# Layer 2 of the last image: its depthwise taps on the unnormalised input, in half chunks, behind layer 1's last products

## The chip, the core and the metric

One core of one Trainium2 chip runs the whole kernel. The metric is the device time of one execution in microseconds; several executions are made, and their median is compared. An execution with the hardware profiler on gives the page and the trace that this document reads; its times are microseconds from its first instruction.

## The reference, cut to what matters

Eight images x of 384 channels and 32 x 32 points go through four residual layers, `x = x + layer_k(group_norm(x))`. Layer 0 is a convolution with attention, layer 1 a mixture of four two-layer networks per point, layer 3 a deformable attention. Layer 2 is what the change touches:

```
h = (x - mean) / sqrt(var + 1e-5)          # per image, 32 groups of 12 channels
y = depthwise 3x3 convolution of h          # ternary weights, zero padding of one point
x = x + (1x1 convolution of y, 384 -> 384)  # ternary weights
```

A group's mean and variance come from all points of the image, so h is known only when the last channel of x is complete. The taps are linear: on a point inside the image, taps of h are scale times (taps of x) plus shift times (sum of the nine taps). On the border some of the taps fall on padding, which is zero in h and not in x.

## The kernel before, in words

A partition holds three channels ("chunks" c = 0, 1, 2) of 1024 points each. Everything is float32. A 128x512 product of TensorE appears in the profile as two MATMUL records.

Work of layers 1 to 3 runs as generators that are interleaved. `layer1(b)` gives a list of units: for each half h of the points (512 of them) 12 groups of three hidden products (`ph`, L1481, with Relu on ACT and a multiplication by the gate on DVE, L1467), then for each output chunk m four parts of three products into `y` (L1502). The last part of a chunk adds the result to x (L1508, DVE). While `layers(b)` (layer 2, then layer 3 of image b) runs, each of its steps yields an estimate of idle time, and units of layer 1 of image b + 1 are put in for it (UNIT = 2.6). For the last image, 7, no later image is left: its layers run against the second part of layer 3 of image 6, two of its steps for each step of the other (`following`, L1995).

`layer2` takes the statistics (`gn_start`, L101: two `bn_stats` a chunk; `gn_finish`, L138: two one-column products `gna`, L117, and `gnb`, L128, with small DVE operations and a power on GpSimd, L98), lets ACT write the normalised image h2 (`affine`, L147), and takes nine taps a chunk on DVE: the centre as `tensor_scalar` (L1569), eight as `scalar_tensor_tensor` (L1577). Then 18 products with the 1x1 weights (`pw`, L1585) and the addition to x (L1592).

`layer3` normalises x again, multiplies it (`pq`, L1622, gives q; `px`, L1645, transposes it to `xT`), takes 25 strided taps of q on DVE (`off`, L1690 and L1692; 54 operations an image and a start), a Gelu on ACT (L1697), products `pom` (L1718), tanh and the interpolation weights `wt` on ACT and GpSimd (L1753 to L1757), the sampling products `xsb` (L1761), keys `pk` (L1775) and values `pv` (L1784), six units of attention (`s` L1800, exp on ACT L1817, `pav` L1826, sums `pss` L1839, transposes and a division on DVE L1847 to L1874) and the output products `pf` (L1929).

Buffers that matter: five image buffers (`im`, 12 KB a partition each); two accumulators of two banks (`big`), three of one bank (`fbank`), one (`vbank`, used by `pav`). The instruction order on each engine is fixed when the program is built; an engine never passes a waiting instruction.

`weights23` prepares the weights of layers 2 and 3 once, in the routing stage of layer 1 (L1346 to L1371).

Of the kernel before, what the change touches and what calls it, by code (L numbers as in the profile page):

```python
# [7 lines left out]
F32 = mybir.dt.float32  # L8
AF = mybir.ActivationFunctionType
ALU = mybir.AluOpType  # L10
AX = mybir.AxisListType

B, C, H, W = 8, 384, 32, 32
N = H * W
# [41 lines left out]
def tile_kernel(ctx: ExitStack, tc: tile.TileContext, i: dict, out: bass.AP):  # L56
# [52 lines left out]
    def gn_mean(st, tag):  # L109
        mv = small.tile([P, 2], F32, tag="gn_mv", name=f"mv_{tag}")  # L110
        nc.vector.bn_aggr(mv, st.rearrange("p a b -> p (a b)"))
        return mv

    def gn_spread(mv, tag, psum):

        pg = psum(f"gna_{tag}")
        nc.tensor.matmul(pg[:, 0:2], lhsT=g4, rhs=mv, start=True, stop=True)  # L117
        ga = small.tile([P, 2], F32, tag="gn_ga", name=f"ga_{tag}")
        nc.vector.tensor_copy(ga, pg[:, 0:2])
        dm = small.tile([P, 1], F32, tag="gn_dm", name=f"dm_{tag}")  # L120
        nc.vector.tensor_tensor(dm, mv[:, 0:1], ga[:, 0:1], ALU.subtract)
        nc.vector.tensor_tensor(dm, dm, dm, ALU.mult)
        return ga, dm
# [14 lines left out]
    def gn_finish(st, tag, psum):  # L138

        return gn_scale(*gn_spread(gn_mean(st, tag), tag, psum), tag, psum)  # L140
# [1196 lines left out]
    def weights23(pl):  # L1337

        raw2 = pl.img("raw2").rearrange("p c n -> p (c n)")
        pw2 = raw2[:, : KC * C].rearrange("p (c n) -> p c n", c=KC)  # L1340
        dw2 = raw2[:, KC * C : KC * C + KC * 9].rearrange("p (c n) -> p c n", c=KC)
        nc.sync.dma_start(out=pw2, in_=i["pw2"])
        nc.sync.dma_start(out=dw2, in_=i["dw2"])
        m2 = wd.tile([P, KC], F32, name="m2")
        s2 = wd.tile([P, KC], F32, name="s2")
        nc.vector.tensor_reduce(m2, dw2, AX.X, ALU.add, apply_absolute_value=True)  # L1346
        nc.vector.tensor_scalar(m2, m2, 1.0 / 9.0, 1e-5, ALU.mult, ALU.max)
        nc.vector.reciprocal(s2, m2)
        tap2 = wd.tile([P, KC, 9], F32, name="tap2")
        ternary(tap2, dw2, [s2[:, c : c + 1] for c in range(KC)])  # L1350
        nc.vector.reciprocal(m2, s2)
        for c in range(KC):
            nc.vector.tensor_scalar(tap2[:, c, :], tap2[:, c, :], m2[:, c : c + 1], None, ALU.mult)
        mp = wd.tile([P, 1], F32, name="mp")
        sp = wd.tile([P, 1], F32, name="sp")
        nc.vector.tensor_reduce(mp, pw2, AX.XY, ALU.add, apply_absolute_value=True)
        pm = fbank("pm")
        nc.tensor.matmul(pm[:, 0:1], lhsT=ones, rhs=mp, start=True, stop=True)
        nc.vector.tensor_scalar(mp, pm[:, 0:1], 1.0 / (C * C), 1e-5, ALU.mult, ALU.max)
        nc.vector.reciprocal(sp, mp)  # L1360
        upw2 = wd.tile([P, KC, C], F32, name="upw2")
        ternary(upw2, pw2, sp)
        nc.vector.reciprocal(mp, sp)
        so3 = wd.tile([P, 1], F32, name="so3")
        bo3 = wd.tile([P, 1], F32, name="bo3")

        nc.vector.tensor_scalar(bo3, bn3[:, 4:5], 1e-6, None, ALU.add)
        rsqrt(so3, bo3, 1)
        nc.vector.tensor_tensor(so3, so3, bn3[:, 1:2], ALU.mult)
        nc.vector.tensor_tensor(bo3, bn3[:, 0:1], bn3[:, 3:4], ALU.subtract)  # L1370
        nc.vector.scalar_tensor_tensor(bo3, bo3, so3, bn3[:, 2:3], ALU.mult, ALU.add)  # L1371
        return tap2, upw2, mp, so3, bo3

# [12 lines left out]
    def third(pl, k, name):  # L1388

        return pl.one([P, KC, HALF], f"hd{k}", name)  # L1390
# [9 lines left out]
    def layer1(pl, b, late=False):  # L1400
# [95 lines left out]
        def result(h, m, part):  # L1496
            if part == 0:
                state["y"] = fbank(f"y{b}_{h}_{m}")
            y = state["y"]
            for k in range(3 * part, 3 * part + 3):  # L1500
                e, dc = divmod(k, KC)
                nc.tensor.matmul(  # L1502
                    y, lhsT=w2[:, e, dc, m * P : (m + 1) * P], rhs=state[h, k],
                    start=(k == 0), stop=(k == NE * KC - 1),
                )
            if part == 3:
                hs = slice(h * HALF, (h + 1) * HALF)
                nc.vector.scalar_tensor_tensor(  # L1508
                    xt[:, m, hs], y, yb[:, 1, m : m + 1], xt[:, m, hs], ALU.add, ALU.add
                )  # L1510

        units = []

# [33 lines left out]
                        unit((result, h, m, part))  # L1547
        return units

    def layer2(pl, b, xt):  # L1550
        last = b == B - 1
        st = None
        for c in range(KC):
            st = gn_start(xt, f"d2_{b}", c, st)
            yield 1.3
        ss = gn_finish(st, f"d2_{b}", fbank if last else vbank)
        yield 5.0
        h2 = pl.img(f"h2_{b}")
        if last:
            y = [third(pl, c, f"y_{b}_{c}").rearrange("p a n -> p (a n)")[:, :N] for c in range(KC)]  # L1560
        else:
            y = pl.img(f"y_{b}")
            y = [y[:, c, :] for c in range(KC)]
        for c in range(KC):
            affine(h2[:, c, :], xt[:, c, :], ss)
        for c in range(KC):
            src = h2[:, c, :].rearrange("p (h w) -> p h w", h=H)
            dst = y[c].rearrange("p (h w) -> p h w", h=H)
            nc.vector.tensor_scalar(dst, src, tap2[:, c, 4:5], None, ALU.mult)  # L1569
            yield 0.8  # L1570
            for t in (0, 1, 2, 3, 5, 6, 7, 8):
                dy, dx = t // 3 - 1, t % 3 - 1
                r0, r1 = max(0, -dy), H - max(0, dy)
                c0, c1 = max(0, -dx), W - max(0, dx)
                d = dst[:, r0:r1, c0:c1]
                f = src[:, r0 + dy : r1 + dy, c0 + dx : c1 + dx]
                nc.vector.scalar_tensor_tensor(d, f, tap2[:, c, t : t + 1], d, ALU.mult, ALU.add)  # L1577
                yield 1.25
        yield 3.5
        for m in range(KC):  # L1580
            whole, pw = pair(last, f"pw{b}_{m}")
            for h in range(2):
                hs = slice(h * HALF, (h + 1) * HALF)
                for c in range(KC):
                    nc.tensor.matmul(  # L1585
                        pw[h], lhsT=upw2[:, c, m * P : (m + 1) * P], rhs=y[c][:, hs],
                        start=(c == 0), stop=(c == KC - 1),
                    )
            xm = xt[:, m, :]
            outs = zip((xm[:, :HALF], xm[:, HALF:]), pw) if last else [(xm, whole)]  # L1590
            for d, f in outs:
                nc.vector.scalar_tensor_tensor(d, f, mp, d, ALU.mult, ALU.add)  # L1592
            nc.sync.dma_start(out=x2_dram[b, :, m, :], in_=xm)
            yield 0.0
# [373 lines left out]
    with pd:  # L1968
        for k, u in enumerate(units):
            u()  # L1970
            if k == 8:
                tap2, upw2, mp, so3, bo3 = weights23(pl)
        def layers(b):
            xt = xs_img.pop(b)
            yield from layer2(pl, b, xt)
            yield from layer3(pl, b, xt, put_image(b), False)

        for b in range(B - 1):
            units = layer1(pl, b + 1)
            due = 0.0  # L1980
            this = layers(b)
            for idle in this:
                if idle is None:
                    if b == B - 2:
                        break
                    continue
                due += idle
                while due >= UNIT and units:
                    units.pop(0)()
                    due -= UNIT  # L1990
            for u in units:
                u()


        following = layers(B - 1)  # L1995
        for _ in this:
            for _ in range(2):
                next(following)
        for _ in following:
            pass  # L2000
        okt = pl.flat([P, B * NU3 * 16], "okt3")
        recf = rec3.rearrange("p u q -> p (u q)")
        nc.vector.tensor_scalar(okt, recf, R_LO, None, ALU.is_ge)
        nc.vector.scalar_tensor_tensor(okt, recf, R_HI, okt, ALU.is_le, ALU.mult)
        okm = pl.one([P, 1], "okm", "okm3")
        nc.vector.tensor_reduce(okm, okt, AX.X, ALU.min)
        pok = fbank("pok3")
        nc.tensor.matmul(pok[:, 0:1], lhsT=ones, rhs=okm, start=True, stop=True)
        nc.vector.tensor_scalar(bad3, pok[:, 0:1], P - 0.5, None, ALU.is_lt)
# [163 lines left out]
```

## Time and profile before

| what | us |
|---|---|
| median of 3 runs | 3491.53 (3490.93 to 3492.99) |
| the profiled execution, its own time | 3494.72 |
| the span of its instructions | 3492.9 |
| TensorE busy (PE) | 3384.1, 97% of the span |
| VectorE busy (DVE) | 1696.7, 49% |
| ScalarE busy (ACT) | 1298.5, 37% |
| GpSimd busy (POOL) | 206.1, 6% |
| mean granted TensorE clock | 0.987 |

How to read it: PE is busy nearly all the time, so the shares over the whole span say little; what one change is worth is read in its own stage. Layer 1 of image 7 ends at 3272.85 us in this trace, layer 2 of image 7 lies between 3273 and 3333, layer 3 of images 6 and 7 fills the rest. A busy PE at half clock counts as busy: matmul records are the same in number and take twice as long.

### The profile page before, as it was taken

What the parts mean: (1) busy time and instruction counts of PE and PEld (TensorE: products, weight loads), DVE (VectorE), ACT (ScalarE), POOL (GpSimd) and SP (SyncE); (2) the same over time, 40 slices, a digit from 0 to 9 for tenths busy, and PEclk for the clock granted to TensorE, in tenths of its full rate; (3) what the DMA queues carried; (4) which work ended last, traced back from release to release, by engine and by line L of the source; (5) the groups of instructions that cost most, each with busy time, mean ns of one, the idle gap of its engine ahead of it and who ended that gap; (6) DMA issues with size and microseconds to landing.
All of it is one profiled execution on the core that took longest, in us unless ns stands there. A gap on an engine that the chain in (4) does not pass through costs nothing.

```text
span 3492.9 us, 44919 instructions
## 1 busy us (share of the span) xinstructions
PE 3384.1 (97%) x18599; PEld 1458.3 (42%) x18599; DVE 1696.7 (49%) x2881; ACT 1298.5 (37%) x1514; POOL 206.1 (6%) x231
## 2 busy tenths in 40 slices
PE   6999999999999999998999999999999999999888
PEld 2333434343434343443344445344453444534434
DVE  8942232323232323234366365663656637566573
ACT  5655544444444444433222323313233232232222
POOL 2100000000000000000000200102001020010112
PEclk9999999999999999999999999999999999999898
DMA  9972121212121212123500101101111011110000
GB/s 357 295 205 79 26 79 27 79 26 79 26 79 26 79 27 78 28 79 125 220 24 21 50 39 35 40 21 50 40 35 40 21 50 40 35 39 18 0 37 19
DMA packets 86259, 234.01 MB, mean 67 GB/s; under 512 B 21672, under 2 KB 21896, under 8 KB 79130
## 3 DMA queue, kind: packets, MB, share of 16 engines
q1 hardware_dynamic: 83882, 222.75, 19.9%
q10 hardware_dynamic: 1248, 4.72, 0.3%
q8 instruction: 150, 2.46, 0.3%
q0 software_dynamic: 912, 3.53, 0.3%
q14 instruction: 67, 0.55, 0.1%
HBM read 145.77 MB, written 75.59 MB: 63 GB/s over the span
## 4 chain that ended last, share of the span: by engine, by line
PE 41%; DVE 9%; DMA 1%; ACT 1%; POOL 0%; issue 0%; DVEq 0%; ACTq 0%; POOLq 0%; SPq 0%
PE y L1502 12%; PE ph L1481 10%; DVE y L1577 5%; PE pq L1622 4%; PE pw L1585 3%; PE pf L1929 3%; PE s L1800 2%; PE pav L1826 2%; DVE hd L1467 1%; DMA o<-o 1%; PE pk L1775 1%; PE pv L1784 1%; PE xsb L1761 1%; PE pss L1839 1%; PE plog L1231 1%; DVE off L1692 1%
## 5 line engine op out<-in xcount | busy, mean ns | idle before, releaser
L827 ACT ACTIVATE p<-s 128x1024 f32<-128x1024 f32 x512 | 496.3, 1021 | 365.7 <-PE s L820 365.5
L835 PE MATMUL pav<-p,vt 64*64 64x512 f32 x4096 | 494.7, 588 | 0.0
L1481 PE MATMUL ph<-h,w_sb 128*128 128x512 f32 x1104 | 486.8, 595 | 6.3 <-ACT h L1430 6.3
L1502 PE MATMUL y<-hd,w_sb 128*128 128x512 f32 x1080 | 488.7, 600 | 3.5 <-DVE hd L1467 3.5
L820 PE MATMUL s<-qk,qk 48*64 48x512 f32 x2944 | 355.1, 592 | 0.0
L1481 PEld LDWEIGHTS ph<-h,w_sb 128*128 128x128 f32 x1104 | 207.0, 190 | 267.5 <-issue 249.8
L1502 PEld LDWEIGHTS y<-hd,w_sb 128*128 128x128 f32 x1080 | 199.9, 191 | 248.2 <-issue 235.8
L835 PEld LDWEIGHTS pav<-p,vt 64*64 64x64 f32 x4096 | 168.2, 133 | 273.7 <-issue 273.4
L796 DVE COPY ta<-pav 128x512 f32<-128x512 f32 (+1 forms) x65 | 44.2, 682 | 475.5 <-PE pav L835 475.5
L1491 ACT ACTIVATE hd<-ph,b_sb 128x512 f32<-128x512 f32 x180 | 122.7, 682 | 312.7 <-PE ph L1481 312.7
L1577 DVE SCALAR_TENSOR_TENSOR y<-h,tap,y 128x961 f32<-128x961 f32 (+1 forms) x192 | 233.8, 1241 | 0.6
L574 PE MATMUL pk<-xs,cws_sb 32*32 32x496 f32 (+3 forms) x3840 | 179.4, 601 | 39.4 <-DMA xs<-in_xs_dram 24.8
L1692 DVE SCALAR_TENSOR_TENSOR off<-q,dw_sb,off 128x225 f32<-128x225 f32 (+3 forms) x432 | 211.9, 544 | 1.6
L820 PEld LDWEIGHTS s<-qk,qk 48*64 48x64 f32 x2944 | 109.1, 133 | 211.4 <-issue 190.5
L1817 ACT ACTIVATE p<-s 128x1024 f32<-128x1024 f32 x96 | 96.1, 1023 | 166.5 <-PE s L1800 141.7
L81 DVE COPY qk<-pq 128x512 f32<-128x512 f32 x46 | 31.8, 691 | 251.9 <-PE pq L258 251.9
L1467 DVE TENSOR_TENSOR hd<-hd,cb 128x512 f32<-128x512 f32 x180 | 122.3, 684 | 41.0 <-ACT hd L1491 40.8
L574 PEld LDWEIGHTS pk<-xs,cws_sb 32*32 32x32 f32 (+1 forms) x3840 | 77.7, 111 | 139.4 <-issue 54.0
L1585 PE MATMUL pw<-y,upw 128*128 128x512 f32 x288 | 129.0, 601 | 4.9 <-DVE y L1577 4.9
L1862 POOL TENSOR_TENSOR p<-p,p 128x1024 f32<-128x1024 f32 x48 | 113.0, 2355 | 349.3 <-ACT p L1817 349.3
L820 PE MATMUL s<-ql,ql 48*64 48x512 f32 x1024 | 128.3, 592 | 0.2 <-ACT p L827 0.2
L1929 PE MATMUL pf<-att,wp_sb 128*128 128x512 f32 x288 | 127.6, 598 | 0.5 <-DVE x L1937 0.5
(326 smaller groups left out, 3718.1 us busy)
## 6 DMA issues: line engine op xcount, KB each, us to landing
rqk<-y SPq DMA_DIRECT2D x96, 256.0 KB
g<-rqk SPq DMA_DIRECT2D x96, 256.0 KB
xs<-in_xs_dram SPq DMA_DIRECT2D x56, 384.0 KB
g<-rv SPq DMA_DIRECT2D x48, 256.0 KB
xh<-in_x_dram SPq DMA_DIRECT2D x48, 256.0 KB
f<-in_x_dram SPq DMA_DIRECT2D x24, 512.0 KB
f<-o SPq DMA_DIRECT2D x24, 512.0 KB
o<-ot SPq DMA_DIRECT2D x42, 256.0 KB
```

The costliest lines, as they stand in the source:

```text
L574: nc.tensor.matmul(banks[r][cols[q]].rearrange("p (h w) -> p h w", w=W)[:, :, c0:c1], lhsT=cws[rs, c, 2 * h + g, x, w], rhs=src[rs, :, c0 ...
L820: nc.tensor.matmul(s[64 * k : 64 * k + 64, j * HALF : (j + 1) * HALF], lhsT=kt[r, k0 : k0 + 64], rhs=qt[r, h * HALF : (h + 1) * HALF], sta ...
L827: nc.scalar.activation(p, s, AF.Exp, scale=scale)
L835: nc.tensor.matmul(pav[k][64 * j : 64 * j + 64, :], lhsT=vts[b % 2][r, kc, 2 * hd : 2 * hd + 2, :].rearrange("p a b -> p (a b)"), rhs=p[r, ...
L1467: nc.vector.tensor_tensor(hd, hd, state["cb"], ALU.mult)
L1481: nc.tensor.matmul(ph, lhsT=w1[:, e, c, dc * P : (dc + 1) * P], rhs=state["h1"][c], start=(c == 0), stop=(c == KC - 1),)
L1502: nc.tensor.matmul(y, lhsT=w2[:, e, dc, m * P : (m + 1) * P], rhs=state[h, k], start=(k == 0), stop=(k == NE * KC - 1),)
L1577: nc.vector.scalar_tensor_tensor(d, f, tap2[:, c, t : t + 1], d, ALU.mult, ALU.add)
L1585: nc.tensor.matmul(pw[h], lhsT=upw2[:, c, m * P : (m + 1) * P], rhs=y[c][:, hs], start=(c == 0), stop=(c == KC - 1),)
L1622: nc.tensor.matmul(pq[h], lhsT=wq3[:, c, m * P : (m + 1) * P], rhs=h3[h][:, c, :], start=(c == 0), stop=(c == KC - 1),)
L1692: nc.vector.scalar_tensor_tensor(d, f, dw3[:, t : t + 1], d, ALU.mult, ALU.add)
L1929: nc.tensor.matmul(pf[:, hs], lhsT=wp3[:, pr, m * P : (m + 1) * P], rhs=att[:, pr, hs], start=(pr == 0), stop=(pr == NPAIR3 - 1),)
```

## The change

For image 7 only, `layer1` calls a new function, `convolve`, after each of the six additions to x (chunk m, half h). It takes that half's `bn_stats`, and then the nine taps on x itself, not on the normalised image, on the rows whose neighbours are already complete (15 rows with the first half, 17 with the second), into a new image `y_last`. When the last half is in, `layer2_last` takes the mean and the variance; with the mean it adds the border's sums of taps (nine small DVE additions), and then ACT applies scale and shift in place, the shift multiplied by the sum of the nine taps. `weights23` gets seven small operations that prepare the sums. `layer2` keeps the images 0 to 6; its 1x1 products become a function, `pointwise`. Each `convolve` adds 6.0 to the planner's account, so that more units of layer 1 of image 7 are put in before the next step of image 6 follows; and the last two images are interleaved one step for one instead of one for two.

```
+        sum2 = wd.tile([P, KC], F32, name="sum2")
+        edge2 = wd.tile([P, KC, 8], F32, name="edge2")
+        taps = tap2.rearrange("p c (a b) -> p c a b", a=3)
+        nc.vector.reduce_sum(sum2, tap2, AX.X)
+        for k in range(2):
+            nc.vector.reduce_sum(edge2[:, :, k], taps[:, :, 2 * k, :], AX.X)
+            nc.vector.reduce_sum(edge2[:, :, 2 + k], taps[:, :, :, 2 * k], AX.X)
+            nc.vector.tensor_scalar(
+                edge2[:, :, 4 + 2 * k : 6 + 2 * k], taps[:, :, 2 * k, 0::2], -1.0, None, ALU.mult
+            )
...
+                if b == B - 1:
+                    convolve(pl, xt, m, h)
...
+    ahead = {"time": 0.0}
+
+    def convolve(pl, xt, c, h):
+
+        if not c and not h:
+            ahead["y"] = pl.img("y_last")
+            ahead["st"] = wd.tile([P, 2 * KC, 6], F32, name="st_last")
+        y = ahead["y"]
+        nc.vector.bn_stats(ahead["st"][:, 2 * c + h, :], xt[:, c, h * HALF : (h + 1) * HALF])
+        src, dst = (t[:, c, :].rearrange("p (h w) -> p h w", h=H) for t in (xt, y))
+        lo, hi = ((0, H // 2 - 1), (H // 2 - 1, H))[h]
+        nc.vector.tensor_scalar(
+            dst[:, lo:hi], src[:, lo:hi], tap2[:, c, 4:5], None, ALU.mult
+        )
+        for t in (0, 1, 2, 3, 5, 6, 7, 8):
+            dy, dx = t // 3 - 1, t % 3 - 1
+            r0, r1 = max(lo, -dy), min(hi, H - dy)
+            c0, c1 = max(0, -dx), W - max(0, dx)
+            d = dst[:, r0:r1, c0:c1]
+            f = src[:, r0 + dy : r1 + dy, c0 + dx : c1 + dx]
+            nc.vector.scalar_tensor_tensor(d, f, tap2[:, c, t : t + 1], d, ALU.mult, ALU.add)
+        ahead["time"] += 6.0
+
+    def layer2_last(b, xt):
+
+        y = ahead["y"]
+        ga, dm = gn_spread(gn_mean(ahead["st"], f"d2_{b}"), f"d2_{b}", fbank)
+        edge = wd.tile([P, KC, 8], F32, name="edge_last")
+        nc.vector.tensor_scalar(edge, edge2, ga[:, 0:1], None, ALU.mult)
+        for c in range(KC):
+            dst = y[:, c, :].rearrange("p (h w) -> p h w", h=H)
+            for d, e, axis in (
+                (dst[:, 0 :: H - 1, :], edge[:, c, 0:2], 2), (dst[:, :, 0 :: W - 1], edge[:, c, 2:4], 1)
+            ):
+                nc.vector.tensor_tensor(d, d, e.unsqueeze(axis).to_broadcast(list(d.shape)), ALU.add)
+            d = dst[:, 0 :: H - 1, 0 :: W - 1]
+            nc.vector.tensor_tensor(
+                d, d, edge[:, c, 4:8].rearrange("p (a b) -> p a b", a=2), ALU.add
+            )
+        ss = gn_scale(ga, dm, f"d2_{b}", fbank)
+        sums = wd.tile([P, KC], F32, name="sums_last")
+        nc.vector.tensor_scalar(sums, sum2, ss[:, 1:2], None, ALU.mult)
+        for c in range(KC):
+            nc.scalar.activation(
+                y[:, c, :], y[:, c, :], AF.Identity, bias=sums[:, c : c + 1], scale=ss[:, 0:1]
+            )
+        yield 5.0
+        yield from pointwise(b, xt, [y[:, c, :] for c in range(KC)])
+
     def layer2(pl, b, xt):
-        last = b == B - 1
...
-        ss = gn_finish(st, f"d2_{b}", fbank if last else vbank)
+        ss = gn_finish(st, f"d2_{b}", vbank)
         yield 5.0
         h2 = pl.img(f"h2_{b}")
-        if last:
-            y = [third(pl, c, f"y_{b}_{c}").rearrange("p a n -> p (a n)")[:, :N] for c in range(KC)]
-        else:
-            y = pl.img(f"y_{b}")
-            y = [y[:, c, :] for c in range(KC)]
+        y = pl.img(f"y_{b}")
+        y = [y[:, c, :] for c in range(KC)]
...
         yield 3.5
+        yield from pointwise(b, xt, y)
+
+    def pointwise(b, xt, y):
+
+        last = b == B - 1
...
             xt = xs_img.pop(b)
-            yield from layer2(pl, b, xt)
+            yield from layer2_last(b, xt) if b == B - 1 else layer2(pl, b, xt)
...
                     units.pop(0)()
-                    due -= UNIT
+                    due += ahead["time"] - UNIT
+                    ahead["time"] = 0.0
...
         for _ in this:
-            for _ in range(2):
-                next(following)
+            next(following)
```

## The prediction

> **What bounds the kernel now.** I read the page's slices first, then what PE waited for after 3094 us, then the chain of waits from there to the end, then busy time by windows.
>
> ```profile
> PE   6999999999999999998999999999999999999888
> PEclk9999999999999999999999999999999999999898
> ```
> Beside the start, and one slice in the middle, only the last three slices of PE fall below 9: the end of the kernel, where layer 2 and 3 of image 7 lie. A core bound by PE loses time only where PE waits or its clock is down.
>
> ```profile
> PE xsb L1761 <- POOL wt L1757: 11.3, 2, 7.3
> PE pom L1718 <- ACT off L1697: 7.7, 1, 7.7
> PE pav L1826 <- DVE tu L1874: 4.2, 1, 4.2
> PE pw L1585 <- DVE y L1577: 4.1, 3, 3.0
> ```
> PE's waits (total, times, longest). Two of them have DVE's taps behind them: pw waits for layer 2's, pom for layer 3's.
>
> ```profile
> 3241.95 30.90 PE y L1502 x72
> ...
> 3284.00 16.24 DVE y L1577 x12
> ...
> 3402.91 5.19 DVE off L1692 x14
> 3408.12 1.03 ACT off L1697
> 3409.19 2.07 PE pom L1718 x2
> ```
> The chain (start, us, what) leaves PE when layer 1's last product ends, at 3272.85, and runs over image 7's 27 taps on DVE; later over the 25 taps of layer 3.
>
> ```profile
> 3211.00:3273.00 62.00, 62.00 (x146) 27.44 (x145) 30.13 (x55) 11.84 (x16) 0.00 (x0) 1.00 0.00 0
> 3273.00:3304.00 31.00, 20.14 (x70) 15.03 (x68) 28.91 (x33) 13.04 (x25) 11.46 (x9) 0.67 0.00 0
> ...
> 3395.00:3414.00 19.00, 10.80 (x21) 4.72 (x20) 13.90 (x23) 1.84 (x2) 0.00 (x0) 0.75 0.20 83
> ```
> Columns: length, busy PE, PEld, DVE, ACT, POOL, granted clock. Before 3273 PE is full while DVE is half idle; after it DVE is full and PE is not, at 0.67 of its clock. DVE work moved from the second window into the first is what the change offers.
>
> **What the skill says.** (1) "TensorE: Matmul & The Clock Gate", Part 1: after an idle window of about 3.4 us the clock halves, and about 3.4 us of sustained work give it back. The trace agrees roughly: PE idles from 3276.9, and by windows of 2 us:
> ```profile
> 3280.00:3282.00 2.00, 0.00 (x0) 0.92 0.00 0
> 3282.00:3284.00 2.00, 0.00 (x0) 0.50 0.00 0
> ...
> 3300.00:3302.00 2.00, 2.00 (x4) 0.50 0.00 0
> 3302.00:3304.00 2.00, 1.47 (x4) 0.96 0.00 0
> ```
> Half speed comes 4.7 us after the idling began, and ends 3 us after the pw products began (3299.2); the 12 us of small xsb products between did not end it. Elsewhere it took 5 us (3378.9 to 3384) and 6 (3409.2 to 3415.2). (2) "VectorE: DVE Perf Modes", on the errata: an operation on SBUF pays a fixed extra time, so splitting costs. Here taps of 240 points took 0.39 us start to start, of 961 1.13: a fixed 0.14. (3) "ScalarE: Activation LUTs", the cost of a table load: about 1.28 us; here ACT_TABLE_LOAD took 1.28. Its section on table sets has tanh beside exp.
>
> **The change, part by part.** All dated in the profiled execution (span 3492.9, own time 3494.72, 3.2 above the median). A product of 128x512 is 0.859 us (36 in the 30.90 above). The compiled order of both programs, engine by engine, gives the sequences.
>
> *Weights.* Seven DVE operations of 0.13 to 0.17 (rows of 27 elements there) are 1.1 us, queued ahead of the routing flags `prs`, for which PE waits (3.5 us at 1729.6). DVE idled 0.94 before `prs`: the rest, +0.2, counts; bounds 0 and 1.5, no gain possible.
>
> *Half-chunk taps.* Start to start 0.14 + 0.00103 n: 434 to 544 points give 0.59 to 0.71; the centre tap 0.4. A first half costs 5.4 us, a second 5.9, six 33.8 against 29.8 for the old 27 (0.66 and 1.16 each). If my line is wrong: 0.39 (240) to 1.13 (961) each.
> First halves lie behind PE: y_0_0 ends 3155.9, its taps end 3166.3; in the new order the pw of image 6 starts at 3163.6, its third accumulator needs DVE's evacuation at 3173.9, DVE is there at 3169. The normalisation of image 6 now goes at 3187 between products, its `pq` falls back from 3185 to 3203, its `off` taps from 3202 to 3220 and their end to 3251. The last gate product `hd` on DVE is done at 3243.7, needed at 3249.8. So PE stays full, and layer 1 ends at 3271.5: 3272.85 less the two `px` groups (12 transposes, 1.3 us) that now come later. Cover: 3.7 to 6 us at each step; if it is gone, PE waits by the overrun.
>
> *The wait after layer 1*, from its end: addition 0.8, bn_stats 0.7, centre 0.4, aggregate 0.3, eight taps 5.4, gna's and gnb's small operations 0.8, nine border additions 1.8 (0.2 each; the nearest rows are 0.15 for one element, 0.41 for 256), power and shift 0.9, sums and wake-ups 0.5, ACT on the first chunk 1.3: 12.9. PE has only gna and gnb meanwhile. pw starts at 3284.4 at half clock; 18 products 15.5, + 2.5 for 5 us at half: 3302.4. (Before: 3299.2 to 3332.)
>
> *Image 6's xT.* Five image buffers hold x6, x7, y_last, h3 and q; `xT` must take y_last's, its evacuation waits for pw's end, and two `px` keep both large accumulators till then. After pw: xT 1.2, px, xT, pom (3 x 1.29 on PE), tanh, weights: pom ends 3309.7, xsb starts 5.4 us after the second tanh as it did in the tail before (3414.7 to 3420.1): 3313.9. Then `pq` of image 7 15.5, xsb 5.4 (0.68 each at 3036), `px` 2.6, `pk` 3.9, + 2.2 half clock, + 1.4 evacuations: pk ends 3344.9.
>
> *Attention of image 6 and `off` of image 7.* pk to the first `pav` 11.2 (3311.1 to 3322.3 before). `tu` is queued behind 13.3 us of `off` on DVE, `pav` has one bank: PE waits 1.9, later 1.8 for the third `tu`, and 1.8 behind the Gelu with two table loads on ACT. The sixth pair ends 39.1 after pk, `pf` 15.5: `pom` at 3399.5. The old 7.7 us wait is gone, since the taps end at pk + 28. Before: 3409.2. Gain 9.7.
>
> *Tail.* With the clock up, pom to xsb takes 8.1, not 10.9: 2.8 gained. The order has no table load before image 7's exp any more: 1.2 gained (PE waited 1.2 there).
>
> *Sum:* 9.7 + 2.8 + 1.2 - 0.2 = 13.5 us. As a check, from layer 1's end to image 7's pom: before 136.3 us, of which dense work 94.1; after 128.0 with 95.4, so loss falls from 42 to 32.6. Forecast 3491.5 - 13.5 = **3478.0**.
>
> **The rivals.** *A wait takes the place of the one removed*: attention of image 6 becomes bound by DVE. For: `off` and `tu` share DVE, one bank; before, PE waited 4.2 there and lost 3 more to half clock. Against: it is in my sum with 5.5. If each wait passes 3.5 us, three waits grow by 2 and two drop the clock, 2.5 each: -11, so 3489; span of this case 3483 to 3492.
> *Slower: the clock stays down.* Place: from 3276 to 3340. For: half clock lasted through 12 us of xsb before. Price: the 36 products of pw and pq at 0.859 more each are 31 us, of which 4.7 is counted: +26, so 3504. It decides if work after a wait never fills a window; from about 16 products at half clock beyond my 5 the gain is gone. Against: pw and pq are dense, and pw got it back in 3 us.
> *More gain*: no clock drop at the two late waits, and earlier evacuations: 6 to 9 more, so 3470.
> *The taps' cover in layer 1 fails* (an overrun of 4 us): 3482, inside the main case.
>
> **How the numbers follow.** About 0.2%, 7 us, is what this measurement can tell from no change. Main case 0.66, 3472 to 3484; attention 0.20 (0.06 of it still faster, 0.13 within 7 us, 0.01 slower); clock 0.08, slower; more gain 0.06. So faster 0.78, same 0.13, slower 0.09. The range, 3468 to 3488, takes in the bounds of border additions (1.8 us either way), half clock (3) and table loads.
>
> **What would show it.** Right: layer 1 ends within 2 us of 3271.5 with PE full; no `y` tap after about 3282; pw in one block near 3284 to 3302; pom of image 7 near 3400 and hardly waiting for `off`; no table load after 3430. Wrong: `hd` or `pw` waits on DVE before 3270; a gap over 16 us before pw; clock at 0.5 through pq; `pav` waiting for `tu` more than 8 us in all.

## The result, and the profile after

The changed kernel took 3480.97 us (median of 9 runs, 3475.82 to 3486.36) beside 3490.93 of the kernel before (9 runs, 3488.24 to 3492.99): ratio 0.9973, 95% interval 0.9964 to 0.9982, so 6 to 13 us less. The forecast was 3478.0, with a range of 3468 to 3488. The profiled execution's own time is 3480.29 beside a span of 3478.5.

The span fell by 14.4 us, more than the medians did. The page's slices tell little; TensorE's share is the same, only the two 8s of the clock near the end are gone:

```profile
PE   6999999999999999998999999999999999999888
PEclk9999999999999999999999999999999999999999
```

The second half of image 6's layer 1 starts its products (`ph`) at 2992.49 before and at 2987.06 after: 5.4 us were won up to there, where the two programs have the same instructions, but for `weights23`. Most of that is in PE's waits from 1760 to 3090 us, the first line of the kernel before, the second of the changed one (total, times, longest):

```profile
PE ph L1481 <- ACT h L1430: 6.1, 5, 1.6
```
```profile
PE ph L1491 <- ACT h L1440: 1.5, 2, 0.9
```

Each is among the first products of an image; behind it stands ACT's `h`, behind that DVE's sum with a loaded tile, and that sum waited for the load: 1.68 us before and 0.71 after, in the same place:

```profile
2003.51 1.28 DVE L1427 SCALAR_TENSOR_TENSOR x<-o,bnsc_out,x 128x1024 f32<-128x1024 f32 x1 [1.68 <-DMA o<-o]
```
```profile
2001.65 1.28 DVE L1437 SCALAR_TENSOR_TENSOR x<-o,bnsc_out,x 128x1024 f32<-128x1024 f32 x1 [0.71 <-DMA o<-o]
```

I take that for scatter, not for the change: in the twelve runs below, eleven of which contain the change, the same start lies between 7.4 us ahead of the kernel before and 2.6 behind it. So I measure the change by the **stretch** from that `ph` to the last busy instruction. It is 495.1 us before and 485.9 after: 9.2 less, which fits the medians. Some of the expectations below call this point the start of layer 1 of image 7. Image 7's own first product comes later, at 3101.59 before and 3096.50 after; counted from there, the stretch is 386.0 and 376.5, which is 9.5 less, so the choice changes little. Each stretch is one execution: the changed kernel, profiled twice, has 485.9 and 487.0, so differences of about 1 us are not to be read.

Where in the stretch, by windows (length, busy PE, PEld, DVE, ACT, POOL, granted clock, DMA share, GB/s), the changed kernel from the end of layer 1 on: the wait, `pw`, the `xT` and `pom` of image 6, `xsb` to `pk`, attention, `pf`, the rest up to the end of the span (5.6 us behind the last busy instruction, 5.3 before):

```profile
3266.03:3277.38 11.35, 0.88 (x4) 0.71 (x4) 9.38 (x28) 1.29 (x2) 0.55 (x1) 0.71 0.00 0
3277.38:3294.88 17.50, 17.49 (x36) 7.37 (x36) 7.23 (x10) 2.21 (x2) 0.00 (x0) 0.90 0.15 60
3294.88:3306.62 11.74, 6.17 (x28) 4.17 (x28) 7.39 (x15) 8.57 (x13) 1.09 (x3) 0.93 0.11 45
3306.62:3336.59 29.97, 29.97 (x127) 20.02 (x128) 9.54 (x21) 11.89 (x25) 3.81 (x7) 0.92 0.00 1
3336.59:3383.14 46.55, 35.54 (x132) 11.55 (x131) 44.99 (x69) 17.75 (x17) 14.69 (x6) 0.89 0.00 0
3383.14:3398.70 15.56, 15.56 (x39) 6.95 (x38) 6.74 (x11) 0.00 (x0) 0.00 (x0) 1.00 0.17 69
3398.70:3478.50 79.80, 68.21 (x249) 34.83 (x247) 30.54 (x48) 22.17 (x35) 18.45 (x14) 0.90 0.07 28
```

The fifth line is the one to see: in attention DVE is busy 44.99 of 46.55 us and PE only 35.54. The place where DVE holds PE up has moved, not gone. PE's waits from 3090 us on say where it stands now:

```profile
PE pav L1888 <- DVE tu L1936: 9.5, 3, 6.1
PE pw L1647 <- ACT y_last L1605: 6.3, 1, 6.3
PE xsb L1823 <- POOL wt L1819: 6.3, 2, 4.1
PE gnb_d L128 <- DVE dm_d L122: 3.5, 2, 2.0
PE gna_d L117 <- DVE mv_d L111: 2.2, 1, 2.2
...
PE pom L1780 <- DVE xT L81: 0.6, 1, 0.6
```

The 7.7 us in which `pom` waited for `off` are gone, `xsb` waits 6.3 instead of 11.3, but `pav` waits 9.5 for `tu` where it waited 4.2. (`tu` is DVE's transpose of what `pav` left in its one bank; until it is done, the next unit's `pav` can't start.) My own sign of a failed step, over 8 us there, is met. What DVE does ahead of the first `tu`, one instruction at a time (start, us), and GpSimd beside it:

```profile
3345.19 2.95 DVE L1754 SCALAR_TENSOR_TENSOR off<-q,dw_sb,off 128x720 f32<-128x720 f32 x1
...
3348.18 2.94 DVE L1754 SCALAR_TENSOR_TENSOR off<-q,dw_sb,off 128x720 f32<-128x720 f32 x1
...
3351.15 1.02 DVE L1754 SCALAR_TENSOR_TENSOR off<-q,dw_sb,off 128x768 f32<-128x768 f32 x1
```
```profile
3344.99 2.39 POOL L1924 TENSOR_TENSOR p<-p,p 128x1024 f32<-128x1024 f32 x1 [25.94 <-ACT p L1879]
...
3347.45 2.89 POOL L1924 TENSOR_TENSOR p<-p,p 128x1024 f32<-128x1024 f32 x1
```

A tap of 720 points takes 2.95 us here and 0.97 in layer 1; one of 768, right behind them, its usual 1.02. The long taps start while GpSimd adds the halves of `p`, and end 0.8 us after its end. The Trainium skill, "SBUF — State Buffer", section "SBUF: two separate sides", states why: an operation of DVE with two SBUF inputs and a GpSimd operation that reads SBUF exclude each other on a port that the two engines share; one goes first, "the other fully blocks". A tap reads q and its own sum, both in SBUF, the memory that holds the tiles. The trace agrees, and in both directions: GpSimd's second addition, which began 0.7 us before the first long tap ended, took 2.89 us, the four after it 2.35 or 2.36. I had not priced that.

### The profile page after: what moved, and what is told of

It is laid out like the page before. It is cut to its first block, busy times and chain, and to the rows that moved or that the text cites. A ratio compares the mean times of both kernels' runs of the same rounds, so it can differ in the third digit from the quotient of the medians.

```text
span 3478.5 us, 44959 instructions
## 1 busy us (share of the span) xinstructions
PE 3372.7 (97%) x18599; PEld 1449.4 (42%) x18599; DVE 1708.2 (49%) x2926; ACT 1298.5 (37%) x1514; POOL 200.1 (6%) x231
## 4 chain that ended last, share of the span: by engine, by line
PE 43%; DVE 8%; DMA 1%; ACT 1%; POOL 0%; issue 0%; DVEq 0%; POOLq 0%; ACTq 0%; SPq 0%
PE y L1512 12%; PE ph L1491 10%; DVE y L1634 4%; PE pq L1684 4%; PE pw L1647 3%; PE pf L1991 3%; PE s L1862 2%; PE pav L1888 2%; DVE off L1754 1%; PE xsb L1823 1%; DVE hd L1477 1%; PE pss L1901 1%; PE pk L1837 1%; PE pv L1846 1%; PE plog L1231 1%; DMA o<-o 1%
## 5 line engine op out<-in xcount | busy, mean ns | idle before, releaser
L1491 PE MATMUL ph<-h,w_sb 128*128 128x512 f32 x1104 | 487.0, 595 | 1.9 <-ACT h L1440 1.8
L1634 DVE SCALAR_TENSOR_TENSOR y<-h,tap,y 128x961 f32<-128x961 f32 (+1 forms) x168 | 203.0, 1229 | 0.5
L711 PE MATMUL pv<-wv_sb,g 128*128 128x384 f32 x384 | 127.1, 489 | 0.0
```

The source lines that it names most:

```text
L711: nc.tensor.matmul(pv[:, :C], lhsT=acts[b][2][:, c, t * P : (t + 1) * P], rhs=w_in[2][:, c, :], start=(c == 0), stop=(c == KC - 1),)
L1491: nc.tensor.matmul(ph, lhsT=w1[:, e, c, dc * P : (dc + 1) * P], rhs=state["h1"][c], start=(c == 0), stop=(c == KC - 1),)
```

## The experiments

**Theory** ("held port"): the shortfall is time in which DVE stands behind GpSimd's additions, on the path because taps and `tu` share DVE. **Rivals**: the mere number of taps queued ahead of `tu`; the image buffer that `y_last` holds; the interleave rather than the taps.

All kernels are timed against the kernel before; the stretch comes from the one profile that each has.

| run | median | ratio (95%) | stretch |
|---|---|---|---|
| before | 3490.9 to 3493.0 | 1 | 495.1 |
| the change | 3480.97 | 0.9973 (0.9964 to 0.9982) | 485.9 |
| e5, the change again | 3485.14 | 0.9980 (0.9973 to 0.9987) | 487.0 |
| e1, no addition of p | 3479.31 | 0.9958 (0.9945 to 0.9972) | 478.3 |
| e2, last taps held | 3488.88 | 0.9991 (0.9983 to 0.9999) | 487.5 |
| e3, xT elsewhere | 3491.0 | 0.9993 (0.9985 to 1.0002) | 494.3 |
| e4, interleave alone | 3510.45 | 1.0046 (1.0032 to 1.0059) | 511.5 |
| e6, sums on TensorE | 3479.62 | 0.9969 (0.9958 to 0.9980) | 481.3 |
| e7, e6 and e2 | 3480.59 | 0.9966 (0.9954 to 0.9979) | 482.1 |
| e8, whole chunks | 3485.36 | 0.9976 (0.9968 to 0.9984) | 487.8 |
| e9, no border sums | 3483.67 | 0.9974 (0.9964 to 0.9983) | 485.6 |
| e10, buffer later | 3481.68 | 0.9968 (0.9956 to 0.9980) | 482.2 |
| e11, e10 and e6 | 3474.45 | 0.9950 (0.9936 to 0.9964) | 477.4 |
| e12, addition on DVE | 3478.34 | 0.9962 (0.9948 to 0.9976) | 481.1 |

**e1: take GpSimd's addition away.**

```
-                p01 = pl.flat([P, N], f"p01_{b}_{u}")
-                nc.gpsimd.tensor_tensor(p01, ps[0], ps[1], ALU.add)
+                p01 = ps[0]
+                if b != B - 2:
+                    p01 = pl.flat([P, N], f"p01_{b}_{u}")
+                    nc.gpsimd.tensor_tensor(p01, ps[0], ps[1], ALU.add)
```


> Leaves out, for image 6 alone, GpSimd's addition of the two halves of the weights p: the sums are taken over the first half. The order of every other instruction stays. Theory 'held port': in the changed kernel six operations of DVE that read two tensors of SBUF took 1.5 to 2.0 us too long while GpSimd's addition (2.36 us) ran, two of them among the 26 taps in front of the first tu. Without the additions no tap of image 7 exceeds 1.1 us, the first wait of pav for tu falls from 6.1 to about 2, the others to under 1, the half clock behind it goes, and the kernel takes 3473 (3470 to 3476), 8 less than the changed kernel. Rival 'queue': the 26 taps alone set the wait; 3479 to 3482, and pav still waits about 9 in all.

The order of DVE's instructions stays the same. 53 of image 7's 54 additive taps by shape (the first one lies earlier), in the changed kernel and in this one (count, busy us, mean ns):

```profile
L1754 DVE SCALAR_TENSOR_TENSOR off<-q,dw_sb,off 128x225 f32<-128x225 f32 x26 | 11.6, 494 | 0.0
L1754 DVE SCALAR_TENSOR_TENSOR off<-q,dw_sb,off 128x720 f32<-128x720 f32 x6 | 9.8, 1627 | 0.2
L1754 DVE SCALAR_TENSOR_TENSOR off<-q,dw_sb,off 128x240 f32<-128x240 f32 x18 | 8.7, 543 | 0.0
L1754 DVE SCALAR_TENSOR_TENSOR off<-q,dw_sb,off 128x768 f32<-128x768 f32 x3 | 3.0, 1005 | 0.1
```
```profile
L1754 DVE SCALAR_TENSOR_TENSOR off<-q,dw_sb,off 128x225 f32<-128x225 f32 x26 | 10.1, 429 | 0.0
L1754 DVE SCALAR_TENSOR_TENSOR off<-q,dw_sb,off 128x240 f32<-128x240 f32 x18 | 7.1, 455 | 0.0
L1754 DVE SCALAR_TENSOR_TENSOR off<-q,dw_sb,off 128x720 f32<-128x720 f32 x6 | 5.8, 969 | 0.2
L1754 DVE SCALAR_TENSOR_TENSOR off<-q,dw_sb,off 128x768 f32<-128x768 f32 x3 | 3.0, 1004 | 0.1
```

33.1 us become 26.0; no shape has long ones any more. The 26 taps ahead of the first `tu` last 13.54 us instead of 17.49; the difference is the 3.95 us by which the two long taps exceeded 0.97:

```profile
3343.60 13.54 DVE L1754 SCALAR_TENSOR_TENSOR off<-q,dw_sb,off 128x240 f32<-128x240 f32 x26
```

`pav`'s wait falls from 9.5 to 2.1, attention from 46.55 to 38.87, and every other window stays within 0.3 us:

```profile
PE pav L1888 <- DVE tu L1938: 2.1, 1, 2.1
```
```profile
3312.48:3342.49 30.01, 30.01 (x127) 20.03 (x128) 9.52 (x21) 11.88 (x25) 3.81 (x7) 0.91 0.00 1
3342.49:3381.36 38.87, 34.00 (x133) 10.94 (x132) 35.73 (x69) 17.43 (x17) 0.00 (x0) 0.96 0.00 0
3381.36:3396.91 15.55, 15.55 (x38) 6.96 (x37) 6.69 (x11) 0.00 (x0) 0.00 (x0) 1.00 0.17 69
```

The stretch is 7.7 to 8.8 us shorter than the changed kernel's. The queue of taps is the same, so "the queue alone" is out; and in this stretch of the changed kernel PE never waited for GpSimd's sum itself. The held port is shown to be the cause. Its size is less sure: the median, 3479.31, missed the theory's 3470 to 3476 and lies in the rival's range. It is 13.0 below the kernel before beside it (3492.32), where the change won 10.0 and in e5 7.3, so by the medians the additions cost 3 to 6 us. Two details of the expectation were off as well: five operations, not six, took 1.5 to 2.0 us too long (the sixth 0.3), and one piece of half clock, 3.4 us, stays behind the first wait.

**e2: hold the last taps behind the first `tu`.**

```
+            dwt = ahead["dw3"] if last and 10 <= t != 12 else dw3
...
+                if b == B - 2 and u == 0:
+                    nc.vector.scalar_tensor_tensor(
+                        ahead["dw3"], tu[:, 0, :25], 0.0, dw3[:, :25], ALU.mult, ALU.add
+                    )
```


> Taps from the eleventh on take their weights from a copy that depends on the first tu, so that tu no longer stands behind six long taps. Theory 'held port' and rival 'queue' both expect the first wait of pav (6.1) to go: 3473 to 3476; taps of 2 to 3 us beside GpSimd's additions stay in the trace and cost nothing. Rival 'attention is bound by PE and ACT anyway': 3479 to 3482. If the taps then end too late, pom of image 7 waits for off instead, 3480 or more.

Both theories were wrong on this. The first `tu` came in time, but `pav` waited at the third, fifth and sixth unit instead, 8.0 us in all:

```profile
PE pav L1889 <- DVE tu L1937: 8.0, 3, 3.1
```

The stretch is 487.5: nothing was won by holding these taps. My reading is that no order helps while DVE's total, with the time that it stands behind GpSimd, exceeds PE's; one other order is not enough to show that. The median is 4 us worse than that stretch lets expect; why, one profile doesn't tell, and it stays open.

**e3: another place for image 6's `xT`.**

```
+        elif b == B - 2:
+            t = pl.one([P, KC, HALF], "h1", f"xT_{b}").rearrange("p c n -> p (c n)")
...
+        if b == B - 2:
+            xT[2:] = [pl.flat([P, 2, C], f"xT_{b}_{k}") for k in (2, 3)]
```


> xT of image 6 goes into the buffer of layer 1's h and two small buffers, instead of the image buffer that y_last holds until the pw products end; so px and pom of image 6 lie ahead of pw. Theory 'slot': the 11.3 us after layer 1 are partly filled, the start of pq of image 7 comes 3 us earlier, five groups of xsb are out of the way (3 us) and less is at half clock (2 us): 3474 (3471 to 3477). Rival 'given back at attention': off of image 7 and tu still share DVE, and pav waits longer by what was gained: 3479 to 3482.

A miss, and not a clean test: with another place, the build also moved `off` of image 6. Its first tap starts 28.7 us before layer 1's end and its last ends 3.1 after it (51.7 and 20.7 before it in the changed kernel). So those taps stand among those of `y_last`, `pom` waits for `off`, `gna` stands behind `pom` on PE, and `pw` (which waits for these statistics) starts 26.4 us after layer 1:

```profile
PE gna_d L117 <- DVE mv_d L111: 6.2, 1, 6.2
...
PE pom L1786 <- ACT off L1765: 4.2, 1, 4.2
```

**e4: the interleave without the taps.**

```
-            for _ in range(2):
-                next(following)
+            next(following)
```


> The kernel before, with the two last images interleaved one step for one and nothing else. Theory: the gain comes from the taps that were moved, the interleave alone changes nothing by itself: 3488 to 3494. Rival 'the interleave is the gain': 3478 to 3484.

16 us slower, which neither side expected. Image 6's attention now runs first, image 7's layers hang behind, and their `off` taps end alone:

```profile
PE pom L1718 <- ACT off L1697: 27.0, 1, 27.0
```

With the old taps, two for one was right, and the interleave alone is not the gain. The moved taps with two for one were not run, so what the new interleave adds to the change, or takes from it, is not known.

**e5: the changed kernel again**, with no edit.

> The changed kernel once more, unaltered, beside the others of this call. If its first profile is typical: from the end of layer 1 to the end of the kernel 206.9 us as before, and about 10 us below the kernel before. The 5.4 us by which that profile was ahead before layer 1 of image 7, where nothing was changed, should not repeat: theory 'they are arrival times of loads' expects another number there; rival 'the change causes them' expects 5 again.

From layer 1's end on it takes 208.1 us (206.9 at first): `pw` lasts 18.17 us instead of 17.50 and attention 46.7, with the same waits to 0.1 us. Its median is 7.3 below the kernel before, 2.7 less than the first time. The start of the stretch was 5.5 us ahead of the kernel before again, as the rival had it; but in e1, e2, e8 and e9, which contain the change too, it started 0.5 to 2.6 behind. So the change is not enough to cause it.

**e6: sum both halves on TensorE, for the first four units.**

```
...
+                    p01 = fbank(f"pss3_{b}_{u}")
+                    for j in range(2):
+                        for kc in range(2):
+                            nc.tensor.matmul(
+                                p01[64 * j : 64 * j + 64, :], lhsT=ones[:, :64],
+                                rhs=ps[kc][:, j * HALF : (j + 1) * HALF],
+                                start=(kc == 0), stop=(kc == 1),
+                            )
```


> For the first four of the six units of image 6, GpSimd's addition is dropped and TensorE sums both halves of p itself: 4 x 4 more records, 3.4 us of PE, same results. Theory 'held port': the stretch from layer 1's end to the last instruction, 206.9 in the changed kernel and 199.5 without the additions, becomes 201 to 204; 3 to 6 below the changed kernel. Rival 'queue, or PE bound': the additional products add 3.4: 210.

202.3 from layer 1's end, as the theory has it. `pav` waits 2.4, and no tap is long. TensorE, the engine that bounds the kernel, takes over work and the kernel gets faster: the median is 5.5 us below that of e5. Here and in e12 the build also placed some of DVE's operations in attention otherwise; only e1 keeps their order.

**e7: e6 with the last taps held**, both edits shown above together.

> The sums on TensorE as in the run before, and the last taps held behind the first tu. With the port free DVE has about 43 us of work against 48 of PE in this attention, so holding pays now: 199 to 202 for the stretch. Rival 'DVE's queue sets it whatever the port does': as with the sums alone, 201 to 204, or more.

203.4: not better than e6. The held taps come late enough to meet the fifth unit's addition on GpSimd (one tap of 225 points took 2.16 us), and the fourth `tu` keeps `pav` waiting 3.06 us. Holding these taps brought nothing with the port free either.

**e8: taps by whole chunks.**

```
-        lo, hi = ((0, H // 2 - 1), (H // 2 - 1, H))[h]
+        if h == 0:
+            return
+        lo, hi = 0, H
...
```


> The nine taps of a chunk in one piece behind its second half, not in two. Theory: the chain after layer 1 is on the path, and the last chunk's taps now take 9.7 us instead of 5.7: pw starts 15.4 us after layer 1 instead of 11.35, and with half clock the kernel is 4 to 6 slower than the changed one. Rival 'other work sets the start of pw': within 1.5 of the changed kernel.

`pw` starts 19.9 us after layer 1, later still than forecast, yet the stretch is only 0.8 to 1.9 longer: `y_last` takes its buffer later, `xT` of image 6 has one in time, and `pom` runs in the wait. The medians of e8 and e5 are the same to 0.2 us. So the half chunks in this form win next to nothing; what they gain, the buffer that they hold takes back.

**e9: no border sums.**

```
...
-                nc.vector.tensor_tensor(d, d, e.unsqueeze(axis).to_broadcast(list(d.shape)), ALU.add)
...
```


> Leaves out the nine additions of the border's sums to y_last (the mean's part on the border is missing). Theory: they lie on the chain between layer 1 and pw, 0.07 to 0.2 us each from start to start, 1.2 in all: pw starts 10.1 us after layer 1 instead of 11.35, and the stretch from layer 1's end falls by 1.2. My prediction had 1.8 for them. Rival 'gna, gnb and GpSimd's power set that time, the additions fill gaps': pw at 11.2 to 11.4.

`pw` starts after 8.84 us, 2.5 earlier, twice what the additions take: without them the build also puts the power and the scale ahead of chunk 2's last three taps, and ACT begins with chunk 0. But `pw` then takes 18.76 us instead of 17.50, more of it at half clock, and the stretch is 0.3 to 1.4 shorter.

**e10: the buffer later, half chunks only where they count.**

```
...
+        if h == 0:
+            return
+        if c == 0:
+            ahead["y"] = pl.img("y_last")
+            conv_rows(xt, 2, 0, H // 2 - 1)
+        conv_rows(xt, c, H // 2 - 1 if c == 2 else 0, H)
...
```


> The taps of chunks 0 and 1 whole, behind their second halves, and only chunk 2 in two halves; y_last takes its image buffer later, so that xT of image 6 has one in time and px and pom of image 6 lie ahead of pw, as in the run with whole chunks, but with only 5.7 us of taps left after layer 1. Theory 'the buffer that y_last holds early costs what the half chunks gain': pw within 14 us of layer 1's end with pom ahead of it; from the start of layer 1 of image 7 to the end 480 to 484 us against 486 to 487 in the changed kernel and 487.8 with whole chunks. Rival 'given back in attention': 485 to 488.

482.2, in the range of the theory, though `pw` starts after 17.2 us and not 14: PE waits 6.1 there for the weights of `xsb`. `pav` still waits 9.9. The profiled execution is the fastest of its six; by the medians this kernel is 11.4 us below the one before, 1 to 4 more than the change.

**e11: the edits of e10 and e6**, and the border's sums for all chunks at once:

```
+        dst = y.rearrange("p c (h w) -> p c h w", h=H)
...
+            (dst[:, :, 0 :: H - 1, :], edge[:, :, 0:2], 3), (dst[:, :, :, 0 :: W - 1], edge[:, :, 2:4], 2)
...
```

> As the run before, with the sums of the first four units of image 6 on TensorE, and the border's sums added in three operations for all chunks instead of nine. If both causes are right and add up: 475 to 479 from the start of layer 1 of image 7, some 8 to 11 below the changed kernel. If one takes the other's place: 480 to 483.

477.4, and a median of 3474.45: 17 to 19 us below the kernel before, where the change won 7 to 10. The two causes add up: in the stretch 4 to 5 us for the buffer (e10), another 5 with the sums and the merged border additions, which were not run apart. `pav` waits 3.5 and attention has 42.28 us with PE busy 37.28 and no half clock:

```profile
3336.28:3378.56 42.28, 37.28 (x153) 12.80 (x150) 39.72 (x80) 18.01 (x18) 4.97 (x2) 1.00 0.00 1
```

**e12: the addition on DVE.**

```
-                nc.gpsimd.tensor_tensor(p01, ps[0], ps[1], ALU.add)
+                eng = nc.vector if b == B - 2 and u < 4 else nc.gpsimd
+                eng.tensor_tensor(p01, ps[0], ps[1], ALU.add)
```


> GpSimd's addition of p goes to DVE for the first four units of image 6. Theory 'held port': four additions of 1.2 us replace 7 to 9 us in which DVE stood behind GpSimd: the stretch from layer 1 of image 7 on is 482 to 485, 2 to 4 below the changed kernel. Rival 'DVE's load alone': 4.8 us more on DVE, 489 to 492.

481.1, a little better than expected. Each addition takes 1.2 us on DVE; one tap is held up, for 1.93 us, where four were, and `pav` waits 6.2. Four additions given to the overloaded engine make it finish sooner, since it hardly stands behind the other one any more.

## Why the prediction was right, step by step

The total fell within 3 us of the forecast, and on the side that was forecast; the same kernel once more (e5) won 7.3 us, little more than half of the 13.5. By steps, from layer 1's end, against the seven windows above:

| step | forecast | measured |
|---|---|---|
| start of the stretch to layer 1's end, shorter by | 1.35 | 1.4 (280.36 to 278.97) |
| wait from layer 1 to `pw` | 12.9 | 11.35 |
| `pw` | 18.0 | 17.50 |
| `pw` to `xsb` of image 6 | 11.5 | 11.74 |
| `xsb` to the end of `pk` | 31.0 | 29.97 |
| `pk` to `pom` of image 7 | 54.6 | 62.11 |
| `pom` to the end | 79.9 | 79.80 |

*Weights, cover.* `weights23` cost nothing: PE's wait near 1730 is 3.50 us in both, so my 0.2 was too much. The seven operations took only 0.66 of the 0.94 us that DVE had idled ahead of `prs`, since they start 0.07 us apart where I had added up their lengths. PE stayed full to layer 1's end. Right. Layer 1 ended at 3266.03, outside the 2 us around 3271.5 that I had named as a sign, but only because all of it began 5.4 us earlier.

*The wait after layer 1* was 1.6 shorter than my sum. The chain of waits of the changed kernel shows the terms (start, us):

```profile
3266.07 0.76 DVE x L1518
3266.83 0.02 issue
3266.85 0.69 DVE st_last L1570
...
3271.38 0.18 DVE y_last L1596
...
3275.00 0.56 POOL ss_d L98
...
3276.09 1.25 ACT y_last L1605
```

The addition to x, bn_stats and ACT are as priced (0.8, 0.7, 1.3); a border addition costs 0.07 to 0.18 from start to start, not 0.2.

*Image 6's `xT` behind `pw`* came as the order had it: `pom` waits for `xT`, not `off`. What the page of before could not tell, e8 and e10 did: that this queue costs some 4 us (4 to 5 by e10's stretch, 1 to 4 by its median), which another sequence of the same taps saves.

*Attention.* This is the step that failed: "`tu` is queued behind 13.3 us of `off` on DVE, `pav` has one bank: PE waits 1.9, later 1.8 for the third `tu`". The queue was the one that I had counted, and its own work is 13.54 us (e1). But it lasted 17.5, the waits were 6.05 and 2.77 and then 0.69, and two of them put PE at half clock: 7.5 us above my sum. The term that I had put at nothing is the time in which DVE stands behind GpSimd. In e1, without the additions, `pk` to `pom` takes 54.4 us against my 54.6, so in sum nothing else is missing in that step. The rival "attention of image 6 becomes bound by DVE", with a chance of 0.20, named the place and what follows there: waits past 3.5 us and two drops of the clock, for which it took 11 off the gain. It gave no reason why the waits should grow. Its range, 3483 to 3492, holds the median of e5 (3485.14), the main case that of the first runs.

It stood in the trace of before. There, too, one tap in attention took 2.17 us and another 1.92, beside GpSimd's additions; I read 0.39 from start to start and passed over the few long ones. They even lie on the chain of waits of before, ahead of the `tu` for which `pav` waited 4.2 us:

```profile
3368.75 1.85 DVE off L1692
...
3373.77 4.32 DVE off L1692 x7
3378.09 0.64 DVE tu L1874
```

The two exceed the usual 0.45 by 3.2 us; how much of that the kernel before lost was not tested.

*Tail.* `pom` to `xsb` 8.5 us (forecast 8.1), no table load after 3430: the last one is at 3372.54. Right.

*Slower: the clock stays down.* It did not: `pq` ran at half clock for a few products, 6.6 us instead of 5.2 for the first third.

What saved the total was in part luck: the other steps were 2.9 us better than forecast in all, this one 7.5 worse, so the stretch gained 9.2 instead of 13.5. The span alone would have flattered me: 14.4, of which 5.4 were won before the stretch, most of it arrival times of loads.

## What to carry to other kernels

When DVE becomes the late engine of a stage, list what GpSimd does there before you sum DVE's operations: those with two SBUF inputs can pay GpSimd's remaining time on top, and an addition taken from GpSimd to the busier engine can make the stage shorter (e6, e12). In the trace of before, look at the longest instance of an operation, not only at its mean. A buffer taken early for work that is moved ahead is itself a cost: ask who would have had it, and whether only the last piece has to be ready early (e10).

## What the runs showed of the hardware that I had not expected

- An operation with one SBUF input, or with its input in PSUM (the accumulators), did not stand behind GpSimd. In the changed kernel GpSimd added from 3374.94 to 3377.30 and from 3378.43 to 3380.78. Meanwhile the multiplication of `tu` by `rec`, with two SBUF inputs, took 2.53 us instead of 0.68, while the transpose out of PSUM and the reciprocal of one SBUF tile took their usual time:

```profile
3375.31 2.53 DVE L1912 TENSOR_TENSOR tu<-tu,rec 128x512 f32<-128x512 f32 x1
...
3378.70 0.72 DVE L1936 STREAM_TRANSPOSE tu<-pav 128x512 f32<-128x512 f32 x1
...
3380.04 0.25 DVE L1911 RECIPROCAL rec<-ts 128x16 f32<-128x16 f32 x1
```

- The half clock comes in pieces of 3.4 us: in the clock records of these traces its stretches after 3100 us, but the one that the end cuts off, last 3.4, 6.8, 10.2, 13.7, 17.1, 20.5 or 27.3 us. In each of the fourteen traces all changes of the clock, from the first to the last, lie on one grid of 3.413 us. The Trainium skill, "TensorE: Matmul & The Clock Gate", Part 1, says that the window by which the clock is set is free-running, and the traces agree. It would explain why `pw` took 17.50 us after 11.35 us of waiting in one execution and 18.17 after the same wait in the next. A wait shortened by 2.5 us (e9) gave back about half of that or less.
